# One visit of small tiles instead of two, and an earlier norm, in the last stage of a fused four-layer kernel

## The chip, the cores and the metric

The kernel runs as one program on one core of one Trainium2 chip. The metric is the device time of an execution in microseconds (us). The core's engines are TensorE (PE in the profile, with its weight loads as PEld), VectorE (DVE), ScalarE (ACT), GpSimd (POOL) and SyncE (SP), whose queue issues most of the transfers.

## The reference

Four layers follow each other on 4096 tokens (64 sequences of 64) of width 256. All are conditioned on one vector of 64 per sequence, here `t`.

```python
x = L0(x, t)     # quantized feed-forward
x = L1(x, t)     # attention, then the gated feed-forward below
x = L2(x, t)     # layer norm, scale and bias with a tanh term
x = L3(x, t)     # adapter whose weights depend on t

# second half of L1
h = gamma(t) * rmsnorm(x) + beta(t)
x = x + alpha(t) * ((silu(h @ gate_w.T) * (h @ hidden_w.T)) @ out_w.T + out_b)
# L2
out = (x - mean) * rsqrt(var + 1e-5) * weight + bias + tanh(t @ lin_w.T + lin_b)
x = out * weight + bias
# L3, with its own 128x256 and 256x128 matrices for each sequence
Wd_b = Wd + 0.1 * (t @ Wdd.T + bdd)
Wu_b = Wu + 0.1 * (t @ Wdu.T + bdu)
x = x + relu(x @ Wd_b.T + bd) @ Wu_b.T + bu
```

The feed-forward of L1 has 1024 hidden units. Its products are made from pairs of rounded high and low parts, three matmuls for each (`mm3`, lines 83 to 85).

## The kernel before, in words

The kernel has three stages: L0, attention, and a last stage that holds the feed-forward of L1 together with L2 and L3. The change lies in the last stage alone. The order of the work on PE, ACT, DVE and POOL is the order in which the program is written. SP's transfers are placed by a planner, which keeps each within its dependences.

The last stage works on eight blocks (`NBLK`) of 512 tokens, which are eight sequences each. A block takes eight steps, one for each 128 hidden units. The loop at line 1032 runs over `n`, with `i` the block and `f` the step in it (`n = 8 * i + f`). Beside the feed-forward of block `i` it carries the work of the blocks before and after it:

- `f_inner(n)` makes the gate and hidden products ("gh", 12 matmuls of 512 columns), takes the Silu on ACT (L695) and multiplies on DVE (L696, "sg"). `f_parts(n)` splits the result into "hhi" (ACT, L717) and "hlo" (DVE, L718). `f_outer(n - 2)` adds the output products of two steps before to "acc" (12 matmuls of 256 columns).
- For the next block: `f_load` (L658) brings its tokens, `f_begin` takes the squares (ACT, L210) and the inverse root of their means (POOL, L201 and L203), `f_scale` scales the rows (ACT, L225, tile "xn"), and `norm_turn` transposes them on PE (L234), multiplies on DVE (L237, "xg") and adds on POOL (L238). One step later the result is split into "xh" and "xl" (L217, L218). The turns stand in steps 5 and 6.
- For the block before: `f_scaled`, `f_added`, `f_stats` and `f_center` (L741, L746, L751, L752, L758, L760) do the residual and the layer norm in steps 1 and 2; `f_adapt` turns it in steps 4 and 5 (PE L794, DVE L795, tile "x4"). Then comes the adapter: `f_down` (PE L824, ACT relu L828, tile "dn") in step 6, `f_up_products` (PE L839) in step 7 and `f_up_store` (DVE L854, tile "yo", and the output transfer L856).
- `f_weights` loads the adapter's matrices ("wd" L771, "wu" L774) and `f_common` adds the common part to them on POOL (L785). `f_base` adds a bias row to the tokens on POOL (L679).

The adapter's products use only half of the array's columns at a time: 32 products of 64 tokens for the down half, 32 for the up half (each is two matmuls in the profile, 64 in all), all with `tile_position=(0, 64 * s)`. All other matmuls of the stage take the full array.

PSUM has eight banks: four for "gh", two for "acc", two for "mm". The two "mm" banks are taken in turn by the transposes and by the adapter's products. The tiles "dn" and "yo" have one buffer each, "wd" and "wu" four (two blocks). "x1" has five, which the loaded tokens and the layer norm's result share.

Two blocks differ. In block 0 there is no block before. In the last block there is no next one; the adapter of block 6 and all of block 7 are done in `f_last`, after the loop.

Of the kernel before, what the change touches and what calls it, by code (L numbers as in the profile page):

```python
# [8 lines left out]
F32 = mybir.dt.float32  # L9
# [8 lines left out]
P = 128  # L18
NB = 64
L = 64  # L20
D = 256
NTOK = NB * L
T = 512
NBLK = NTOK // T
# [3 lines left out]
BN = 128  # L28
# [8 lines left out]
def tile_kernel(ctx: ExitStack, tc, xT, x, condT, cw, upT, downT, qkvT, woT, ghT, outT_w,  # L37
                vecs, rows, g1, g2, gb, out):
    nc = tc.nc
# [8 lines left out]
    s1d = dram.tile([2, NB, 128, BN], F32, name="s1d")  # L48
    s2d = dram.tile([2, NB, 64, D], F32, name="s2d")
# [12 lines left out]
    def bank(tag):  # L62
        uid[0] += 1
        tags = pools["tags"]
        if tag not in tags:
            tag = "mm"
        return pools["ps"].tile([P, 512], F32, tag=tag, bufs=tags[tag], name=f"{tag}_{uid[0]}")
# [6 lines left out]
    def block(name):  # L74
        return main.tile([P, TT, D], F32, tag="x1", bufs=X1, name=name)

    def tok(ap, i):

        return ap[i * T:(i + 1) * T, :].rearrange("(t p) d -> p t d", p=P)
# [126 lines left out]
    def rms(xb, name):  # L206
        ss = main.tile([P, TT], F32, tag="ss", bufs=2, name=f"ss{name}")
        for t in range(TT):
            junk = main.tile([P, D], F32, tag="junk", bufs=1, name=f"junk{name}_{t}")
            nc.scalar.activation(junk, xb[:, t], AF.Square, accum_out=ss[:, t:t + 1])  # L210
        return rsqrt(ss, 1.0 / D, 1e-6, name)
# [8 lines left out]
    def norm_tm(xb, rs, name, scalar=False):  # L220

        xn = main.tile([P, TT, D], F32, tag="xn", bufs=1, name=f"xn{name}")
        for t in range(TT):
            if scalar:
                nc.scalar.activation(xn[:, t], xb[:, t], AF.Copy, scale=rs[:, t:t + 1])  # L225
            else:
                nc.vector.tensor_scalar(xn[:, t], xb[:, t], rs[:, t:t + 1], None, ALU.mult)
        return xn, parts(name)
# [427 lines left out]
    def f_load(i):  # L656
        x2 = block(f"fx2_{i}")
        nc.sync.dma_start(out=x2, in_=tok(x2d, i))  # L658
        fblk[i] = dict(x2=x2)

    def f_begin(i):
        fblk[i]["rs"] = rms(fblk[i]["x2"], f"f{i}")

    def f_scale(i):
        fblk[i]["n"] = norm_tm(fblk[i]["x2"], fblk[i]["rs"], f"f{i}", i > 0)
# [88 lines left out]
    def f_center(i, tiles, rs):  # L754

        B, n, t0 = fblk[i], len(tiles), tiles[0]
        nm = pools["c"].tile([P, TT], F32, tag="nm", bufs=2, name=f"nm{i}_{t0}")
        nc.vector.scalar_tensor_tensor(nm[:, :n], B["mv"][:, t0:t0 + n, 0], -1.0, rs[:, :n], ALU.mult, ALU.mult)  # L758
        for k, t in enumerate(tiles):
            nc.scalar.activation(B["x3"][:, t], B["x3"][:, t], AF.Identity, bias=nm[:, k:k + 1], scale=rs[:, k:k + 1])  # L760

    def f_weights(i):

        pool = pools["c"]
        B = fblk[i]
        B["wd"], B["wu"] = [], []
        for k in range(2):
            bs = slice(i * BB + 4 * k, i * BB + 4 * k + 4)
            wd = pool.tile([P, 4, 2, BN], F32, tag="wd", bufs=4, name=f"wd{i}_{k}")
            for c in range(2):  # L770
                nc.sync.dma_start(out=wd[:, :, c, :], in_=s1d[c, bs].rearrange("b d n -> d b n"))  # L771
            wu = pool.tile([P, 4, D], F32, tag="wu", bufs=4, name=f"wu{i}_{k}")
            for s in range(2):
                nc.sync.dma_start(out=wu[s * 64:(s + 1) * 64], in_=s2d[s, bs].rearrange("b n d -> n b d"))  # L774
            B["wd"].append(wd)
            B["wu"].append(wu)

    def f_common(i, which, k):

# [35 lines left out]
    def f_down(i, half=None):  # L815
        B = fblk[i]
        if half in (None, 0):
            B["dn"] = pools["c"].tile([P, T], F32, tag="dn", bufs=1, name=f"dn{i}")
        b0, b1 = (0, BB) if half is None else (half * BB // 2, (half + 1) * BB // 2)
        pd = bank("mm" if half is None else "acc")  # L820
        for b in range(b0, b1):
            for c in range(2):
                for s in range(2):
                    nc.tensor.matmul(pd[s * 64:(s + 1) * 64, (b - b0) * L:(b - b0 + 1) * L],  # L824
                                     lhsT=B["wd"][b // 4][:, b % 4, c, s * 64:(s + 1) * 64],
                                     rhs=B["x4"][:, c, b * L:(b + 1) * L], start=c == 0, stop=c == 1,
                                     tile_position=(0, 64 * s))
        nc.scalar.activation(B["dn"][:, b0 * L:b1 * L], pd[:, :(b1 - b0) * L], AF.Relu, bias=vc[:, 5, 0:1])  # L828

    def f_up_products(i, half=None):  # L830
        B = fblk[i]
        b0, b1 = (0, BB) if half is None else (half * BB // 2, (half + 1) * BB // 2)
        pus = []
        for c in range(2):
            pu = bank("mm" if half is None else "gh")
            for b in range(b0, b1):
                for s in range(2):
                    o = c * P + s * 64
                    nc.tensor.matmul(pu[s * 64:(s + 1) * 64, (b - b0) * L:(b - b0 + 1) * L],  # L839
                                     lhsT=B["wu"][b // 4][:, b % 4, o:o + 64],  # L840
                                     rhs=B["dn"][:, b * L:(b + 1) * L], start=True, stop=True,
                                     tile_position=(0, 64 * s))
            pus.append(pu)
        return pus

    def f_up_store(i, pus, half=None):
        B = fblk[i]
        if half in (None, 0):
            B["yo"] = pools["c"].tile([P, 2, T], F32, tag="yo", bufs=1, name=f"yo{i}") if i + 1 < NBLK else \
                main.tile([P, 2, T], F32, tag="xn", bufs=1, name=f"yo{i}")  # L850
        yo, n = B["yo"], T if half is None else T // 2
        o = 0 if half is None else half * n
        for c in range(2):
            nc.vector.scalar_tensor_tensor(yo[:, c, o:o + n], pus[c][:, :n], vc[:, 4, c:c + 1], B["x4"][:, c, o:o + n],  # L854
                                           ALU.add, ALU.add)
            nc.sync.dma_start(out=out[c * P:(c + 1) * P, i * T + o:i * T + o + n], in_=yo[:, c, o:o + n])  # L856
# [86 lines left out]
    for w in range(W):  # L943
        i, tp = divmod(w, 2)
# [86 lines left out]
    late = []  # L1031
    for n in range(5, N):
        i, f = divmod(n, 8)
        ahead = 0 < i < NBLK - 1

        for rest in late:
            rest()
        late = []
        if i > 0 and f == 2:
            f_added(i - 1, 1)  # L1040
            f_stats(i - 1, 1)
            rln = rsqrt(fblk[i - 1]["mv"][:, :, 1], 1.0, 1e-5, f"ln{i - 1}")
        sg = f_inner(n)
        if i > 0 and f in (4, 5):
            f_adapt(i - 1, f - 4)
        if i + 1 < NBLK and f in (5, 6):
            late = [norm_turn(*fblk[i + 1]["n"], i + 1, f - 5, V_FG, V_FB)]
        if ahead and f == 6:
            f_down(i - 1)
        if ahead and f == 7:  # L1050
            pus = f_up_products(i - 1)
        f_parts(n, sg)
        f_outer(n - 2) if n > 5 else None
        if ahead and f == 7:
            f_up_store(i - 1, pus)
        if n == 6:
            for k in range(2):
                nc.vector.scalar_tensor_tensor(bias[:, k], gbt[:, 2 * k + 1], 0.1, gbt[:, 2 * k], ALU.mult, ALU.add)
        if i > 0:
            if f == 1:  # L1060
                for k in range(2):
                    f_scaled(i - 1, k)
                f_added(i - 1, 0)
                f_stats(i - 1, 0)
            if f == 2:
                f_center(i - 1, range(TT), rln)
        if f == 2 and i > 0:
            f_rows(i)
            if i + 1 < NBLK:
                f_load(i + 1)  # L1070
        if i > 0 and i + 1 < NBLK:
            if f == 3:
                f_begin(i + 1)
            if f == 4:
                f_scale(i + 1)

        if f == (6 if i + 1 < NBLK else 2):
            f_weights(i)
        if i + 1 < NBLK and f == 7:
            f_common(i, "wd", 0)  # L1080
            f_base(i)
        if i > 0 and f == 0:
            f_common(i - 1, "wd", 1)
        if i > 0 and f in (3, 4):
            f_common(i - 1, "wu", f - 3)
        if i + 1 == NBLK:
            if f == 4:
                f_base(i)
            if f in (5, 6):
                f_common(i, "wd", f - 5)  # L1090
                f_common(i, "wu", f - 5)
# [57 lines left out]
```

## Time and profile before

| | us |
|---|---|
| Median of three runs | 783.71 |
| Lowest and highest run | 780.1 and 784.03 |
| The profiled execution | 783.55 |
| Its span, from first to last instruction | 781.8 |
| PE busy | 755.3 (97% of the span) |
| DVE, ACT, POOL busy | 546.0, 398.0, 342.1 |
| The last stage from 474 us on: PE busy | 301.2 of 308.0 |

The granted TensorE clock is 0.995 in the mean. Matmuls overlap in the profile: [...]the next matmul starts earlier. So PE's busy share hides short waits, and the distance from start to start tells what a matmul costs the engine. A line of a timeline gives the start, the duration, engine, line and operation, output and inputs, shapes, and the number of instructions merged into it.

### The profile page before, as it was taken

To read this page: it belongs to the slowest core of one execution; us is meant where nothing else is said; L and a number is where in the kernel's file an instruction comes from. 1 tells how busy PE (TensorE), PEld (TensorE's weight loads), DVE (VectorE), ACT (ScalarE), POOL (GpSimd) and SP (SyncE) were. 2 spreads that over 40 slices of the span, in tenths; PEclk is the share of its full clock that TensorE was granted. 3 is DMA by queue.
4 is the path that set the end of the run, shared out by engine and by line. 5 is a ranking of instruction groups with operands and counts; after the bars stand their busy time and mean duration, and the time that the engine had idled before them with its cause. 6 is when DMAs were issued, how large, how long until landed. Compare 5 with 4: busy or idle time off the path is not lost. (4 is left out here: it accounts for less than half of the span.)

```text
span 781.8 us, 17390 instructions
## 1 busy us (share of the span) xinstructions
PE 755.3 (97%) x7014; PEld 615.7 (79%) x7014; DVE 546.0 (70%) x859; ACT 398.0 (51%) x818; POOL 342.1 (44%) x352
## 2 busy tenths in 40 slices
PE   4999999999999989999999999999999999999997
PEld 3677776776777878888788888888888888888886
DVE  4677687777678678998888886555655555464565
ACT  4624345344354478888778664434334352526242
POOL 4311121221324236666556416380818273645491
PEclk9998999999999999999999999999999999999999
DMA  9987988997974783554663137725161616161501
GB/s 322 273 154 215 269 230 223 292 211 208 284 195 117 174 191 84 141 141 139 150 150 92 42 115 176 162 65 152 55 162 55 162 56 162 55 163 33 157 1 55
DMA packets 117136, 118.87 MB, mean 152 GB/s; under 512 B 39568, under 2 KB 100624, under 8 KB 117056
## 3 DMA queue, kind: packets, MB, share of 16 engines
q1 hardware_dynamic: 109024, 91.35, 47.9%
q0 software_dynamic: 7488, 25.37, 9.1%
q8 instruction: 55, 0.90, 0.5%
q10 hardware_dynamic: 544, 1.05, 0.4%
q14 instruction: 25, 0.20, 0.1%
HBM read 71.41 MB, written 29.56 MB: 129 GB/s over the span
## 5 line engine op out<-in xcount | busy, mean ns | idle before, releaser
L83 PE MATMUL mm<-up,xhl 128*128 128x512 f32 x256 | 107.6, 420 | 2.2 <-ACT xhl L217 2.2
L696 DVE TENSOR_TENSOR sg<-gh,sg 128x512 f32<-128x512 f32 x61 | 42.0, 688 | 93.5 <-ACT sg L695 47.4
L84 PE MATMUL mm<-up,xhl 128*128 128x512 f32 x256 | 103.5, 404 | 0.5 <-DVE up L308 0.5
L85 PE MATMUL mm<-up,xll 128*128 128x512 f32 x256 | 102.9, 402 | 0.0
L83 PE MATMUL gh<-xhf,gh 128*128 128x512 f32 x244 | 97.2, 399 | 0.0
L84 PE MATMUL gh<-xlf,gh 128*128 128x512 f32 x244 | 96.9, 397 | 0.0
L85 PE MATMUL gh<-xhf,gh 128*128 128x512 f32 x244 | 96.9, 397 | 0.0
L374 ACT ACTIVATE g<-mm,rs_l 128x512 f32<-128x512 f32 x64 | 44.0, 689 | 90.0 <-PE mm L85 61.9
L718 DVE TENSOR_TENSOR hlo<-sg,hhi 128x512 fp32r<-128x512 f32 x61 | 63.1, 1035 | 37.0 <-ACT hhi L717 36.6
L717 ACT CAST hhi<-sg 128x512 fp32r<-128x512 f32 x61 | 37.8, 619 | 84.7 <-DVE sg L696 83.8
L375 DVE SCALAR_TENSOR_TENSOR h<-mm,rs_l,g 128x512 f32<-128x512 f32 x64 | 47.6, 746 | 44.6 <-PE mm L85 43.5
L83 PE MATMUL acc<-wout,hhi 128*128 128x256 f32 x256 | 74.9, 293 | 0.0
L85 PE MATMUL acc<-wout,hlo 128*128 128x256 f32 x256 | 72.4, 283 | 0.3 <-DVE hlo L718 0.2
L84 PE MATMUL acc<-wout,hhi 128*128 128x256 f32 x256 | 72.3, 282 | 0.0
L83 PEld LDWEIGHTS mm<-up,xhl 128*128 128x128 f32 x256 | 49.4, 193 | 25.6 <-DVE am L383 4.9
L695 ACT ACTIVATE sg<-gh 128x512 f32<-128x512 f32 x61 | 36.0, 590 | 53.2 <-PE gh L85 53.2
L85 PEld LDWEIGHTS mm<-up,xll 128*128 128x128 f32 x256 | 49.2, 192 | 12.3 <-DVE xll L218 0.5
L84 PEld LDWEIGHTS mm<-up,xhl 128*128 128x128 f32 x256 | 49.4, 193 | 11.5 <-DVE up L308 1.2
L238 POOL TENSOR_TENSOR xg<-xg,cv 128x512 f32<-128x512 f32 x32 | 35.8, 1127 | 43.7 <-DVE xg L237 43.7
L85 PEld LDWEIGHTS gh<-xhf,gh 128*128 128x128 f32 x244 | 46.1, 189 | 10.8
L84 PEld LDWEIGHTS gh<-xlf,gh 128*128 128x128 f32 x244 | 46.3, 190 | 8.1
L83 PEld LDWEIGHTS gh<-xhf,gh 128*128 128x128 f32 x244 | 46.3, 190 | 8.1
(188 smaller groups left out, 1879.7 us busy)
## 6 DMA issues: line engine op xcount, KB each, us to landing
gt<-in_g SPq DMA_DIRECT2D x32, 512.0 KB, 5.6
rows<-alphad SPq DMA_DIRECT2D x48, 256.0 KB, 4.2
s1d<-stg POOLq DMA_DIRECT2D x32, 256.0 KB, 6.7
s2d<-stg POOLq DMA_DIRECT2D x32, 256.0 KB, 6.5
vb<-vx SPq DMA_DIRECT2D x32, 256.0 KB, 4.7
wd<-s1d SPq DMA_DIRECT2D x32, 256.0 KB, 4.2
wu<-s2d SPq DMA_DIRECT2D x32, 256.0 KB, 5.8
xf<-in_xT SPq DMA_DIRECT2D x8, 512.0 KB, 3.8
```

Of the source, the lines that this page charges most:

```text
L83: nc.tensor.matmul(out, lhsT=l[0], rhs=r[0], start=first, stop=False)
L84: nc.tensor.matmul(out, lhsT=l[0], rhs=r[1], start=False, stop=False)
L85: nc.tensor.matmul(out, lhsT=l[1], rhs=r[0], start=False, stop=last)
L238: nc.gpsimd.tensor_tensor(b3(xg), b3(xg), bc(vb, c, i), ALU.add)
L374: nc.scalar.activation(g, pg, AF.Gelu, scale=rs[:, t:t + 1])
L375: nc.vector.scalar_tensor_tensor(h[:, ch * 512:(ch + 1) * 512], pv, rs[:, t:t + 1], g, ALU.mult, ALU.mult)
L695: nc.scalar.activation(sg, pg, AF.Silu)
L696: nc.vector.tensor_tensor(sg, pv, sg, ALU.mult)
L717: nc.scalar.copy(h_hi, sg)
L718: nc.vector.tensor_tensor(h_lo, sg, h_hi.bitcast(F32), ALU.subtract)
```

## The change

It has two parts, both in the loop at line 1032.

The norm of the next block moves ahead: its load from step 2 to step 0, its squares from step 3 to step 1, its scales from step 4 to step 3. The two turns stay in steps 5 and 6.

The adapter's two halves share a place: in step 7 of block `i` PE makes half of the up products of block `i - 2`, then the down products of block `i - 1`, then the other half of the up products. The up half is thus a block later than before. `f_up_products` gets a function that it calls between its halves, and `f_up_store` can store one half. The last up half of the loop (block 5) comes in step 0 of block 7. The weight loads are parted: "wd" in step 6 and "wu" in step 7, and in the last block both in step 1 instead of step 2.

```diff
-    def f_weights(i):
+    def f_weights(i, which):
...
-    def f_up_products(i, half=None):
+    def f_up_products(i, half=None, between=lambda pus: None):
...
             pu = bank("mm" if half is None else "gh")
+            pus.append(pu)
             for b in range(b0, b1):
...
-            pus.append(pu)
+            if c == 0:
+                between(pus)
         return pus
 
-    def f_up_store(i, pus, half=None):
+    def f_up_store(i, pus, half=None, chunks=range(2)):
...
-        for c in range(2):
+        for c in chunks:
...
-        ahead = 0 < i < NBLK - 1
+        more = i + 1 < NBLK
...
-        if i + 1 < NBLK and f in (5, 6):
+        if more and f in (5, 6):
             late = [norm_turn(*fblk[i + 1]["n"], i + 1, f - 5, V_FG, V_FB)]
-        if ahead and f == 6:
+        up = i - 2 if more and f == 7 else i - 2 if not more and f == 0 else -1
+        if up >= 0:
+
+            def between(pus):
+                f_up_store(up, pus, chunks=range(1))
+                if more:
+                    f_down(i - 1)
+            pus = f_up_products(up, between=between)
+            f_up_store(up, pus, chunks=range(1, 2))
+        elif more and i > 0 and f == 7:
             f_down(i - 1)
-        if ahead and f == 7:
-            pus = f_up_products(i - 1)
         f_parts(n, sg)
         f_outer(n - 2) if n > 5 else None
-        if ahead and f == 7:
-            f_up_store(i - 1, pus)
...
+        if i > 0 and more:
+            if f == 0:
+                f_load(i + 1)
+            if f == 1:
+                f_begin(i + 1)
+            if f == 3:
+                f_scale(i + 1)
         if f == 2 and i > 0:
             f_rows(i)
-            if i + 1 < NBLK:
-                f_load(i + 1)
-        if i > 0 and i + 1 < NBLK:
-            if f == 3:
-                f_begin(i + 1)
-            if f == 4:
-                f_scale(i + 1)
-
-        if f == (6 if i + 1 < NBLK else 2):
-            f_weights(i)
-        if i + 1 < NBLK and f == 7:
+
+        if f == (6 if more else 1):
+            f_weights(i, "wd")
+        if f == (7 if more else 1):
+            f_weights(i, "wu")
+        if more and f == 7:
             f_common(i, "wd", 0)
             f_base(i)
```

More of the change, by code (lines that the diff above doesn't have):

```diff
@@ L760, in f_center @@
             nc.scalar.activation(B["x3"][:, t], B["x3"][:, t], AF.Identity, bias=nm[:, k:k + 1], scale=rs[:, k:k + 1])
-    def f_weights(i):
+    def f_weights(i, which):
         pool = pools["c"]
         B = fblk[i]
-        B["wd"], B["wu"] = [], []
+        B[which] = []
         for k in range(2):
             bs = slice(i * BB + 4 * k, i * BB + 4 * k + 4)
-            wd = pool.tile([P, 4, 2, BN], F32, tag="wd", bufs=4, name=f"wd{i}_{k}")
-            for c in range(2):
[L771 to L776, printed above, removed]
+            if which == "wd":
+                w = pool.tile([P, 4, 2, BN], F32, tag="wd", bufs=4, name=f"wd{i}_{k}")
+                for c in range(2):
+                    nc.sync.dma_start(out=w[:, :, c, :], in_=s1d[c, bs].rearrange("b d n -> d b n"))
+            else:
+                w = pool.tile([P, 4, D], F32, tag="wu", bufs=4, name=f"wu{i}_{k}")
+                for s in range(2):
+                    nc.sync.dma_start(out=w[s * 64:(s + 1) * 64], in_=s2d[s, bs].rearrange("b n d -> n b d"))
+            B[which].append(w)
     def f_common(i, which, k):
@@ L842, in f_up_products @@
                                      tile_position=(0, 64 * s))
-            pus.append(pu)
+            if c == 0:
+                between(pus)
         return pus
-    def f_up_store(i, pus, half=None):
+    def f_up_store(i, pus, half=None, chunks=range(2)):
         B = fblk[i]
-        if half in (None, 0):
+        if half in (None, 0) and chunks[0] == 0:
             B["yo"] = pools["c"].tile([P, 2, T], F32, tag="yo", bufs=1, name=f"yo{i}") if i + 1 < NBLK else \
@@ L852, in f_up_store @@
         o = 0 if half is None else half * n
-        for c in range(2):
+        for c in chunks:
             nc.vector.scalar_tensor_tensor(yo[:, c, o:o + n], pus[c][:, :n], vc[:, 4, c:c + 1], B["x4"][:, c, o:o + n],
@@ L1085, in tile_kernel @@
             f_common(i - 1, "wu", f - 3)
-        if i + 1 == NBLK:
+        if not more:
             if f == 4:
```

## The prediction

> **What bounds the kernel now.** Names: step f of block i is one pass of the last loop (n = 8i + f); a *visit* is a stretch in which TensorE leaves the full array for the 128x64 tiles of L824 (down) or L839 (up). I read the page for the whole, then the table of busy times by stretch for the last stage, cut at the starts of one block's step 7 to the next:
>
> ```profile
> PE 755.3 (97%) x7014; PEld 615.7 (79%) x7014; DVE 546.0 (70%) x859; ACT 398.0 (51%) x818; POOL 342.1 (44%) x352
> ...
> 520.60:561.30 40.70, 40.56 (x338) 35.16 (x337) 21.85 (x35) 16.75 (x35) 20.92 (x19) 1.00 0.39 104
> 561.30:602.00 40.70, 40.56 (x338) 35.16 (x337) 21.82 (x35) 16.76 (x35) 20.92 (x19) 1.00 0.40 102
> ```
>
> A block takes 40.7 us and PE is busy for 40.56 of it, while DVE has 21.8, ACT 16.8, POOL 20.9. Only what TensorE issues, or waits for, sets the stage. Busy time hides short waits, since matmuls overlap; so next the waits of the weight loads from 485 us on:
>
> ```profile
> PEld mm L234 <- ACT xnf L225: 3.1, 12, 0.3
> PEld mm L839 <- issue: 2.2, 6, 0.4
> ...
> PEld mm L824 <- POOL xg L238: 1.0, 6, 0.2
> ```
>
> The first is the wait that the norm's move aims at; the other two recur six times at the entry of visits. Their true price is in start times, in PE's timeline. An undisturbed turn of the norm, a stalled one (step 5), a down visit (step 6), an up visit (step 7):
>
> ```profile
> 477.92 0.60 PE L234 MATMUL mm<-ident,xnf 128*128 128x128 f32 x4
> 478.27 0.36 PE L83 MATMUL acc<-wout,hhi 128*128 128x256 f32 x1
> 478.48 0.28 PE L84 MATMUL acc<-wout,hhi 128*128 128x256 f32 x1
> ...
> 549.55 1.21 PE L234 MATMUL mm<-ident,xnf 128*128 128x128 f32 x4
> 550.51 0.36 PE L83 MATMUL acc<-wout,hhi 128*128 128x256 f32 x1
> ...
> 554.82 0.60 PE L234 MATMUL mm<-ident,xnf 128*128 128x128 f32 x4
> 555.35 2.09 PE L824 MATMUL mm<-x,wd 128*64 128x64 f32 x64
> 557.36 0.38 PE L83 MATMUL acc<-wout,hhi 128*128 128x256 f32 x1
> 557.59 0.28 PE L84 MATMUL acc<-wout,hhi 128*128 128x256 f32 x1
> ...
> 561.46 0.39 PE L85 MATMUL gh<-xhf,gh 128*128 128x512 f32 x1
> 561.78 2.08 PE L839 MATMUL mm<-dn,wu 128*64 128x64 f32 x64
> 563.80 0.38 PE L83 MATMUL acc<-wout,hhi 128*128 128x256 f32 x1
> 564.02 0.28 PE L84 MATMUL acc<-wout,hhi 128*128 128x256 f32 x1
> ```
>
> The 64 small matmuls follow each other at (2.09 - 0.22) / 63 = 0.0297 us (the last one's own length taken off), 1.90 us in all. The rest of a visit is entry and exit.
>
> **What the Trainium skill says.** "TensorEngine Tiling (Array Packing)", Key Properties: changing the tiling mode, unlike changing the tile, drains TensorE. The trace agrees: entry comes 0.32 us after the last gh start where gh follows gh after 0.23, and the first two acc matmuls after a visit are 0.22 apart instead of 0.12. Up and down both use the 128x64 mode, so between them no drain is due. "SBUF — State Buffer", Who interferes with whom: a VectorE instruction with two SBUF inputs contends with a GpSimd one that reads SBUF. The trace agrees: hlo (L718) takes 0.69 us alone and 1.29 to 1.73 beside POOL's bias adds (L785). "TensorE: Matmul & The Clock Gate", Architectural detail: ScalarE and VectorE are strict first-in, first-out. The trace agrees: xhf (L217) waits 2.98 us for POOL at 555.22 and the Silu behind it starts right after.
>
> **The change, part by part.**
>
> *Norm earlier.* The squares (L210, four, 2.04 us with their reads) go from step 3 to step 1, the scales (L225, four, 1.70 us) from 4 to 3, the load from 2 to 0; nothing is added. The stalled turn takes 550.51 - 549.55 = 0.96 us, the undisturbed one 478.27 - 477.92 = 0.35. Twelve waits are two in each of six turns: 6 x 0.61 = **3.6 us off PE**. Cover for the moved work: between steps 1 and 2 ACT idles 1.48 us ahead of the Silu and 4.04 ahead of hhi, while DVE does the statistics; 2.04 us of squares make that Silu 0.56 late, of 4.04. The scales, in the place of the squares at 544.77, end near 546.5, 3 us ahead of the turn. POOL's ms and rs of the norm (1.2 us) now stand ahead of ms_ln, for which POOL idles 10.86 us.
>
> *Two visits in one.* Step 6 loses its down visit: from turn to second acc 557.59 - 554.82 = 2.77 us becomes 478.48 - 477.92 = 0.56, so -2.21, six times. Step 7 in blocks 2 to 6 gains 64 small matmuls without entry or exit, +1.90 (five times); in block 1 it holds a down in place of an up, 0. Block 7 gains an up visit in step 0: 564.02 - 561.46 = 2.56 against 0.36 for a plain gh to second acc (0.24 + 0.12), +2.20. Sum: -13.3 + 9.5 + 2.2 = **-1.6 us**.
>
> *New waits, and what stands behind them.* Let V be a visit's start.
> - The second up half takes the PSUM bank of the first ("mm" has two), so PE waits for DVE's first yo (L854). That can start at V + 0.95 + 0.19 + 0.04 = 1.18 (products, last one's end, hand-over as at L828), after sg, which ends at V + 0.87 (561.96 + 0.69 - 561.78); it takes 0.74 and ends at V + 1.92. PE wants the bank at V + 0.95 + 1.90 = 2.85. Slack 0.9 us: nothing.
> - "dn" has one buffer, so the relu (L828) waits for the second up half, to V + 4.0, and hhi and hlo of step 7 stand behind it on ACT and DVE, to V + 7.1 at the longest hlo. Their acc products come two steps later: 3.8 + 0.15 + two acc groups of 1.44 + two gh groups of 2.80 = V + 12.4. Slack 5 us.
> - SP: the wd loads no longer wait for a down visit (118.7 us in six waits now); wu waits for the up visit instead, leaves at about V + 4 to 7 and lands 5.8 us later, while POOL touches it after rs_ln at V + 19. The next block's load stands behind it, still most of a block ahead of its squares, against a landing of 7.9 us. In the first block the load of block 2 precedes gbt and waits for a store issued at 448.91; gbt is used at 481.46. The block-7 weights move from step 2 to 1, and are touched in step 5. All nothing.
> - POOL's wu adds (5.5 us) move from beside steps 4 and 5 to beside 2 and 3, where they meet hlo of step 2: it may take 0.9 us more, and nm, centring, Silu of steps 3 and 4 and x4 (L795) follow. The step-5 turn takes the bank that x4 frees: now 548.03 + 0.74 = 548.77 against 549.55, slack 0.78. The scales are 0.34 us shorter than the squares whose place in ACT they take, so 0.78 + 0.34 - 0.9 = 0.2 us is left. This is the tightest place. Bounds: 0, or up to 0.5 us a turn if hlo and Silu lose more, 6 x 0.5 = 3.0. I take 0.
>
> Sum: 783.55 (profiled execution; 781.8 span and 1.75 around it) - 3.6 - 1.6 = **778.4 us**. The median of the runs, 783.71, lies 0.16 above that execution, so the ratio is 0.993 either way. A measurement of this kernel can tell about 0.5% (3.9 us) from no change; the limit is 779.8.
>
> **The rivals.**
> - *The turn waits for DVE instead of ACT* (the last bullet). For it: 0.2 us of slack. Against: hlo's delay is once a block. 778.4 + 3.0 = 781.4.
> - *The norm isn't earlier in fact*: its load or squares run late behind what SP holds, and the scales end where they did. For it: one queue, with a block's weights ahead. Against: the lead of most of a block. Only the visits gain: 782.0.
> - *Slower: the merged visit starves on its bank.* If DVE ends the first yo after V + 2.85, PE stands in the middle of each of five visits. The gain is gone when it ends 0.9 + 5.2 / 5 = 1.9 us later than reckoned. With hlo of step 6 (1.73) running into V and sg behind it, 2.8 late: 5 x 1.9 = 9.5, giving 787.9. Against: now hlo of step 6 ends over 2 us ahead of V.
>
> **How the numbers follow.** Forecast 0.62; bank of the turn 0.20; norm not earlier 0.10; starved visit 0.06; the rest unnamed. The first, and little else, is faster by over 0.5%: 0.64. The two middle ones and part of the forecast's edge are within 0.5%: 0.29. Slower: 0.07. Range: the three runs of before reach 3.6 us below their median, so down to 775.0; upwards it takes in both middle cases, to 782.5. The starved visit is left out.
>
> **What would show it.** Right: a block of 39.8 us between step-7 visits (40.7 - 0.61 - 0.31); no wait of L234 on L225; in step 7 one unbroken stretch of 128 small matmuls, 3.8 us, followed by an acc group. Wrong: L234 waiting on L795, or L839 on L854; small matmuls slower than 0.0297 us where up and down meet; a wait of acc on hlo in steps 0 to 2; or a time above 782.5.

## The result, and the profile after

The changed kernel takes 779.23 us in the median of 20 runs (773.96 to 782.29), beside 782.02 us for 20 runs of the kernel before (776.9 to 784.96). The ratio is 0.9959, with a 95% interval of 0.9944 to 0.9974: 3.2 us faster, between 2.0 and 4.4. Forecast were 778.4 us and a ratio of 0.993. Run again beside other runs of the kernel before, it gave 0.9953 (0.9933 to 0.9973). So the change makes the kernel faster, by about six tenths of the 5.2 us reckoned.

The profiled execution of the changed kernel took 774.54 us with a span of 772.8. That can't be set against the 781.8 of before as it stands. In all profiled kernels of this study PE has the same work in the same order up to the start of block 1 (n = 8), and yet block 1 starts anywhere between 479.1 and 485.7 us. Most of the difference between these two executions goes with TensorE's clock near the start of the program. In that of before the first 512-column matmuls follow each other at 0.43 us until 19.3 us and at 0.23 behind that, and the granted clock is 0.50 from 56.8 to 63.6 us; in that of the changed kernel the change comes at 14.4 us, and the clock is 0.50 from 55.4 to 58.8. So it ran for 8.2 us less at about half the speed. That is worth some 4.1 us (an estimate from these figures) of the 5.0 by which its block 1 starts earlier. So I compare distances inside the last stage, which repeat within 0.02 us a block.

First the busy line of the page, then the table by stretch (length, then PE, PEld, DVE, ACT and POOL, clock, DMA share, GB/s), cut at the merged visits of blocks 2 and 3:

```profile
PE 747.4 (97%) x7014; PEld 612.3 (79%) x7014; DVE 548.1 (71%) x859; ACT 397.4 (51%) x818; POOL 343.9 (45%) x352
```

```profile
551.38:591.16 39.78, 39.78 (x337) 34.96 (x336) 22.37 (x35) 16.67 (x35) 21.13 (x19) 1.00 0.45 107
```

A block takes 39.79 us in place of 40.65, as forecast (39.8), and PE shows no idle time in it: it still sets the pace. The longest waits of the weight loads from 478 us on:

```profile
PEld mm L841 <- issue: 2.2, 6, 0.4
PEld acc L825 <- issue: 1.7, 2, 0.8
PEld mm L841 <- POOL rs_ln L203: 0.9, 1, 0.9
```

The wait of L234 on L225, 3.1 us in twelve waits, is gone, and so is that at the entry of six down visits (1.0 us); six entries with up products stay. The wait on POOL's rs_ln is in the tail, where PE is in truth held by the relu behind the down products: it ends at 759.03, and the up products start at 759.13. Next PE's timeline, the turn of step 5 and the merged visit of step 7:

```profile
541.93 0.63 PE L234 MATMUL mm<-ident,xnf 128*128 128x128 f32 x4
542.31 0.36 PE L83 MATMUL acc<-wout,hhi 128*128 128x256 f32 x1
...
551.06 0.39 PE L85 MATMUL gh<-xhf,gh 128*128 128x512 f32 x1
551.38 1.15 PE L841 MATMUL mm<-dn,wu 128*64 128x64 f32 x32
552.37 2.04 PE L825 MATMUL mm<-x,wd 128*64 128x64 f32 x64
554.23 1.10 PE L841 MATMUL mm<-dn,wu 128*64 128x64 f32 x32
555.27 0.38 PE L83 MATMUL acc<-wout,hhi 128*128 128x256 f32 x1
555.49 0.28 PE L84 MATMUL acc<-wout,hhi 128*128 128x256 f32 x1
```

The turn goes from 541.93 to 542.31, 0.38 us where it was 0.96. The visit is one stretch of 128 small matmuls: 32 up, 64 down, 32 up, from 551.38 to 555.27, that is 3.89 with the exit. From up to down and from down to up the last start and the next are 0.05 us apart: next to nothing is lost where the two meet. Entry (0.32) and the two starts after the exit (0.22 apart) are as before, once a block in place of twice.

### The profile page after: what moved, and what is told of

Read it like the earlier page. It is cut to its first block, busy times and chain, and to the rows that moved or that the text cites. A ratio compares the mean times of both kernels' runs of the same rounds, so it can differ in the third digit from the quotient of the medians.

```text
span 772.8 us, 17369 instructions
## 1 busy us (share of the span) xinstructions
PE 747.4 (97%) x7014; PEld 612.3 (79%) x7014; DVE 548.1 (71%) x859; ACT 397.4 (51%) x818; POOL 343.9 (45%) x352
## 4 chain that ended last, share of the span: by engine, by line
PE 91%; DVE 4%; issue 2%; ACT 1%; DMA 1%; POOL 0%; SPq 0%; DVEq 0%
PE mm L83 12%; PE mm L84 11%; PE mm L85 11%; PE gh L83 7%; PE gh L84 7%; PE gh L85 7%; PE acc L83 4%; PE mm L273 4%; PE acc L85 4%; PE mm L400 4%; PE acc L84 4%; PE mm L591 2%; PE S L550 2%; PE mm L234 2%; PE mm L610 2%
## 5 line engine op out<-in xcount | busy, mean ns | idle before, releaser
L83 PE MATMUL mm<-up,xhl 128*128 128x512 f32 x256 | 106.4, 416 | 2.2 <-ACT xhl L217 2.2
L84 PE MATMUL mm<-up,xhl 128*128 128x512 f32 x256 | 102.1, 399 | 0.5 <-DVE up L308 0.5
L718 DVE TENSOR_TENSOR hlo<-sg,hhi 128x512 fp32r<-128x512 f32 x61 | 58.6, 960 | 31.3 <-ACT hhi L717 30.3
L85 PEld LDWEIGHTS mm<-up,xll 128*128 128x128 f32 x256 | 48.4, 189 | 12.1 <-DVE xll L218 0.5
```

Of the source, the lines that this page charges most:

```text
L83: nc.tensor.matmul(out, lhsT=l[0], rhs=r[0], start=first, stop=False)
L84: nc.tensor.matmul(out, lhsT=l[0], rhs=r[1], start=False, stop=False)
L85: nc.tensor.matmul(out, lhsT=l[1], rhs=r[0], start=False, stop=last)
L718: nc.vector.tensor_tensor(h_lo, sg, h_hi.bitcast(F32), ALU.subtract)
```

## The experiments

The distances below are from the traces. A step's length is taken from its first gate product to the next step's first; step 5 and step 7 are those of block 2; "blocks 1 to 6" is the sum of the six; the end is the distance from the start of the last matmul to the end of the span.

| kernel | step 5 | step 7 | blocks 1 to 6 | block 7, step 0 | end | ratio to before (95%) |
|---|---|---|---|---|---|---|
| before | 5.71 | 6.43 | 243.92 | 4.24 | 3.83 | |
| changed | 5.18 | 8.30 | 236.86 | 6.43 | 4.61 | 0.9959 (0.9944 to 0.9974) |
| norm_only | 5.17 | 6.43 | 240.65 | 4.24 | 3.62 | 0.9959 (0.9944 to 0.9974) |
| visits_only | 5.71 | 8.30 | 240.02 | 6.43 | 4.60 | 0.9996 (0.9976 to 1.0015) |
| split_up | 5.71 | 6.67 | 245.66 | 4.30 | 3.77 | 1.0023 (1.0007 to 1.0038) |
| tail_up | 5.16 | 8.30 | 236.77 | 4.24 | 3.45 | 1.0118 (1.0086 to 1.015) |
| begin_early | 5.10 | 6.43 | 240.25 | 4.24 | 4.07 | 0.996 (0.9944 to 0.9976) |
| store_two | 5.17 | 8.31 | 236.84 | 6.43 | 4.73 | 0.9933 (0.9905 to 0.9962) |
| tail_six_two | 5.16 | 8.31 | 236.85 | 4.24 | 3.51 | 0.9978 (0.9962 to 0.9994) |
| late_yo | 5.16 | 9.33 | 241.94 | 6.43 | 4.40 | 0.9996 (0.9978 to 1.0015) |
| scale_four | 5.11 | 8.30 | 236.43 | 6.43 | 3.96 | 0.9947 (0.9932 to 0.9963) |
| after_again | 5.16 | 8.30 | 236.82 | 6.43 | 4.11 | 0.9953 (0.9933 to 0.9973) |
| more_loads | 5.17 | 8.30 | 236.81 | 6.43 | 4.94 | a single run |

**norm_only: the norm's move alone.** The kernel before with

```diff
+        if i > 0 and i + 1 < NBLK:
+            if f == 0:
+                f_load(i + 1)
+            if f == 1:
+                f_begin(i + 1)
+            if f == 3:
+                f_scale(i + 1)
         if f == 2 and i > 0:
             f_rows(i)
-            if i + 1 < NBLK:
-                f_load(i + 1)
-        if i > 0 and i + 1 < NBLK:
-            if f == 3:
-                f_begin(i + 1)
-            if f == 4:
-                f_scale(i + 1)
```

> Only the norm's move: load in step 0, squares in step 1, scales in step 3; the visits stay as in the kernel before. Theory (the two parts add up, the norm is worth 0.52 to 0.61 us a block): a block goes from 40.65 to about 40.1 us, steps 5 from 5.71 to 5.1 to 5.2, no wait of L234 on the scales, and the kernel is 3.1 to 3.6 us faster than before (ratio about 0.9957). Rival (the wait only ended because the merged visit gave DVE and ACT another order): step 5 stays at 5.7 and the time stays within 1 us of before.

Step 5 fell to 5.17, a block to 40.11, the six blocks by 3.27 us; the ratio says 3.2 us. The move works alone, and takes 0.545 us a block off PE, not 0.61.

**visits_only: the merged visit alone.** The changed kernel with the norm's three calls back in steps 2, 3 and 4.

> Only the merged visit: the norm's load, squares and scales are put back to steps 2, 3 and 4. Theory: step 5 stays at 5.7 us with its wait; blocks 2 to 6 lose 0.31 us each, block 1 loses 2.2, block 7 gains 2.2, so 1.6 us faster than before in the trace (ratio about 0.998). Rival (the last block pays 0.8 us more because of the up visit in step 0 and what it delays): 0.8 us faster only, and the stretch from the last matmul to the end is again about 0.8 us longer than before, as in the changed kernel (4.4 against 3.6 us).

The six blocks lose 3.90 us and step 0 of block 7 gains 2.19: -1.71 us, near the -1.6 reckoned. The last step gives some of it back: PE waits 0.7 us there for an hlo (0.37 more than in the changed kernel), and the end is 4.60. In the time nothing can be seen: the interval reaches from -1.9 to +1.2 us. The two parts add: -3.27 - 1.71 = -4.98, against -7.06 + 2.19 = -4.87 with both.

**split_up: the price of one visit.** The kernel before with its up visit in two:

```diff
+        f_parts(n, sg)
         if ahead and f == 7:
-            pus = f_up_products(i - 1)
-        f_parts(n, sg)
-        f_outer(n - 2) if n > 5 else None
-        if ahead and f == 7:
+            pus = f_up_products(i - 1, between=lambda: f_outer(n - 2))
             f_up_store(i - 1, pus)
+        else:
+            f_outer(n - 2) if n > 5 else None
```

> The kernel before with its up visit of step 7 cut in two: the first 32 small matmuls, then the acc group, then the other 32. One more entry and exit for each of six blocks, no other work. Theory (a visit costs its entry and exit, 0.31 us beside its matmuls): step 7 goes from 6.43 to about 6.74 us, 1.9 us slower than before in all (ratio 1.0024). Rival (the price of a visit is the wait for its operands, not the change of tiling): step 7 stays within 0.1 us of 6.43.

Step 7 grew by 0.24 and the step behind it by 0.06: 0.30 us for one entry and exit with no other work, 1.74 us over the six blocks, and the ratio gives 1.8. So the 0.31 that the merged visit saves is the change of tiling, not a wait for operands.

**begin_early: which of the moved calls mattered.** The kernel before with only f_load in step 0 and f_begin in step 1; f_scale stays in step 4.

> The kernel before with only the load and the squares of the norm moved ahead (steps 0 and 1); the scales stay in step 4. Theory (what made the turn late was ACT's queue: 2.04 us of squares ahead of the Silu of step 4, so that the scales behind it ended 0.6 us too late): with the squares gone the scales of step 4 end about 1.9 us earlier by themselves, step 5 falls to about 5.17 us as it did with the whole move, 3.2 us faster than before (ratio 0.9957). Rival (it is the place of the scales that counts): step 5 stays at 5.7 us, same time as before.

The turn's stall is gone without touching the scales: step 5 is 5.10, its floor of a plain step and two turns (4.24 + 2 x 0.43), and the six blocks lose 3.67 us, as much as was reckoned for the whole move. ACT's timeline shows why. First the kernel before, then this one; step 5 of block 3 starts at 586.96 and at 586.75:

```profile
587.45 0.58 ACT L695 ACTIVATE sg<-gh 128x512 f32<-128x512 f32 x1
588.79 0.62 ACT L717 CAST hhi<-sg 128x512 fp32r<-128x512 f32 x1 [0.76 <-DVE sg L696]
589.32 1.71 ACT L225 ACTIVATE xnf<-fx,rs_f 128x256 f32<-128x256 f32 x4
```

```profile
586.31 0.59 ACT L695 ACTIVATE sg<-gh 128x512 f32<-128x512 f32 x1
587.76 0.62 ACT L717 CAST hhi<-sg 128x512 fp32r<-128x512 f32 x1 [0.86 <-DVE sg L696]
588.29 1.70 ACT L225 ACTIVATE xnf<-fx,rs_f 128x256 f32<-128x256 f32 x4
```

The scales ended 4.07 us after the step's start before, and 3.24 now, when the turn starts: just in time. The squares had stood ahead of the Silu of step 4 on ACT, and everything behind them was late.

**scale_four: the changed kernel with f_scale in step 4.**

```diff
-            if f == 3:
+            if f == 4:
                 f_scale(i + 1)
```

> The changed kernel with the scales of the norm back in step 4; load and squares stay in steps 0 and 1. Theory (with the squares gone the scales are early enough in step 4, and in step 3 they push the work behind them on ACT and DVE, and with it the first x4, so that the turn of step 5 waits for its bank): step 5 falls from 5.17 to 5.19 to about 5.10 us, 6 x 0.08 = 0.5 us faster than the changed kernel, 0.5% faster than before with what that has. Rival (in the changed kernel POOL's bias adds stand elsewhere than in the kernel before, so the scales of step 4 are late again, or the bank wait has another cause): step 5 stays at 5.17 us or more.

Step 5 is 5.11 and a block 39.71: 0.43 us off the six blocks. What holds the turn of the changed kernel instead of the scales is seen in its timeline, in step 5 of block 3 (starts at 578.43):

```profile
577.99 1.71 ACT L225 ACTIVATE xnf<-fx,rs_f 128x256 f32<-128x256 f32 x4
...
579.60 0.58 ACT L695 ACTIVATE sg<-gh 128x512 f32<-128x512 f32 x1
580.21 0.69 DVE L696 TENSOR_TENSOR sg<-gh,sg 128x512 f32<-128x512 f32 x1 [1.40 <-ACT sg L695]
580.82 0.74 DVE L796 SCALAR_TENSOR_TENSOR x<-mm,w,cv 128x512 f32<-128x512 f32 x1
...
581.71 0.63 PE L234 MATMUL mm<-ident,xnf 128*128 128x128 f32 x4
```

The scales in step 3 hold up the Silu of step 4, that the sg, that the x4, which ends at 581.56. The turn takes the bank that x4 has read, starts 0.15 us later, and so 3.28 us into the step, where it starts at 3.24 in begin_early. This is the best version of the study: in the trace it is 0.43 us a stage ahead of the changed kernel, and its ratio to before is 0.9947; that it beats the changed kernel the times can't tell (the intervals overlap).

**late_yo: the slack of the second up half.** The changed kernel with hhi and hlo ahead of the first yo:

```diff
             def between(pus):
+                f_parts(n, sg)
                 f_up_store(up, pus, chunks=range(1))
...
-        f_parts(n, sg)
+        if up < 0:
+            f_parts(n, sg)
```

> The changed kernel with hhi and hlo of the step put ahead of the first yo addition, on ACT and DVE, in each merged visit. It tests the slack of 0.9 us that the second up half has. Theory (PE wants the bank 2.85 us after the visit's start; the first yo ended at 1.96 and now comes behind hhi of 0.62 and hlo of 0.69 to 1.6 us, so at 3.0 to 4.0): PE stands 0.2 to 1.1 us in the middle of each of five visits, step 7 goes from 8.30 to 8.5 to 9.4 us, 1 to 5.5 us slower than the changed kernel. Rival (the bank is not what PE would wait for): step 7 stays at 8.30 us.

PE stands in each of five visits, in the waits of the weight loads and in PE's timeline:

```profile
PEld mm L841 <- DVE yo L857: 4.8, 5, 1.0
```

```profile
555.28 1.15 PE L841 MATMUL mm<-dn,wu 128*64 128x64 f32 x32
556.26 2.04 PE L825 MATMUL mm<-x,wd 128*64 128x64 f32 x64
559.11 1.15 PE L841 MATMUL mm<-dn,wu 128*64 128x64 f32 x32 [0.81 <-DVE yo L857]
```

The second half starts 3.83 us after the visit's start, in place of 2.85. Step 7 is 1.03 longer, the blocks 5.1 us in all; the time is that of the kernel before. The first yo ends 3.78 us into the visit, 1.82 later than in the changed kernel, and PE stands for 0.98 of it. So the slack of 0.9 us that the prediction gave this wait is real and needed: one instruction pair more ahead of the yo on DVE's queue costs the gain. In the changed kernel the yo runs from 552.59 to 553.34, 1.96 us into the visit, as reckoned (1.92).

**tail_up: the odd up visit after the loop.** The changed kernel with

```diff
-        up = i - 2 if more and f == 7 else i - 2 if not more and f == 0 else -1
+        up = i - 2 if more and f == 7 else -1
...
         f_down(i - 1)
+        f_up_store(i - 2, f_up_products(i - 2))
```

in `f_last`, and "dn" of block 6 in a buffer of the sg.

> The changed kernel with the up products of block 5 moved from step 0 of block 7 to after the loop, between the down and the up products of block 6, in the visit that is there in any case, where PE waited 0.8 us for the relu. Theory: step 0 of block 7 falls from 6.43 to 4.24 us; the visit in the tail grows by 1.9 us of small matmuls less the 0.8 us of wait; so about 1.1 us faster than the changed kernel, and nearly 4.3 us faster than before (ratio 0.9945). Rival (the tail is bound by DVE and ACT, and two more yo additions of 0.74 us each on DVE push the turns back): the gain of 2.2 us in step 0 is lost again in the tail, same time as the changed kernel. In either case, if the 0.8 us at the end come from the visit in step 0, the end is back to 3.6 us.

Both were wrong: it is 1.2% slower than before. Step 0 gained its 2.19, and the last step with the tail went from 24.09 to 39.13 us. The longest waits from 740 us on:

```profile
POOL wu L786 <- DMA wu<-s2d: 19.8, 1, 19.8
ACT x L760 <- DVE nm L758: 16.6, 2, 14.7
PEld gh L807 <- ACT x L760: 12.6, 2, 12.2
```

"wu" has buffers for two blocks. Block 5's, now read after the loop, are those that the load of block 7 needs; POOL stands for that load with the bias adds at the head of its queue, the layer norm's root behind them, and PE for the layer norm. Behind that wait the granted clock was at 0.50, from 764.4 to 781.5 us: the two down groups took 2.1 us each, where the changed kernel has 1.38, and the last 64 up products 2.70 in place of 2.04. That is another 2.1 of the 15 us. I had counted engines and forgotten who holds the buffers.

**tail_six_two: down and up in step 6 of block 7.** The changed kernel with

```diff
-        up = i - 2 if more and f == 7 else i - 2 if not more and f == 0 else -1
+        up = i - 2 if f == (7 if more else 6) else -1
```

the load of block 7's "wu" behind that visit, its adds in `f_last` (one before the first root, one after the second), no down products of block 6 there, and the transfers of store_two.

> The changed kernel with the up products of block 5 and the down products of block 6 in one visit in step 6 of block 7 (so none in step 0, and only the up products of block 6 are left after the loop), the up weights of block 7 loaded behind that visit and their bias added beside the layer norm of block 7; and the last transfers on two queues as in the run of that name. The last up products wait for nothing else. Theory: step 0 loses 2.19 us, step 6 gains 3.8 + 0.31; after the loop PE loses the 0.83 us wait for the relu and 1.9 us of down products, but the first turn then waits for the layer norm, so that it starts about 2.2 us earlier than now; net 0.3 us, with the two queues 1.0 to 1.4 us faster than the changed kernel. Rival (the up weights of block 7 come late again, as they did when the up products of block 5 stood after the loop and held their buffers): the last up products wait for POOL, and the kernel is 1 to 6 us slower than the changed one.

The up weights came in time and the last up products did not wait for them, and still it is 3.7 us longer in the stage than the changed kernel. The table by stretch (the eighth figure is the granted clock):

```profile
760.00:762.00 2.00, 1.75 (x61) 1.61 (x56) 1.83 (x6) 0.00 (x0) 0.79 (x2) 1.00 0.00 0
762.00:764.00 2.00, 0.67 (x4) 0.45 (x4) 1.54 (x6) 1.09 (x2) 0.32 (x3) 1.00 0.00 0
764.00:766.00 2.00, 1.38 (x22) 1.15 (x22) 1.68 (x3) 0.04 (x1) 2.00 (x3) 0.59 0.00 0
766.00:768.00 2.00, 2.00 (x22) 1.43 (x19) 0.00 (x0) 1.52 (x3) 1.13 (x1) 0.50 0.00 0
```

The last step's hlo now ran beside the moved wu adds and took 1.64 us, so that PE stood 0.8 us for it. With less work left for it, PE then waited 1.4 us for the layer norm, and from about 764.4 us on the clock was halved. It stayed so to the end of PE's work: the last 64 up products took 3.63 us in place of 2.04, the two down groups 2.11 each in place of 1.38, 3.1 us together. In the changed kernel the tail's 758 to 766 us are busy to 5.9 of 8 us and keep the full clock. The Trainium skill, "TensorE: Matmul & The Clock Gate", Part 1: The HAM clock gate, tells of the halving after an idle window of some 3.4 us. Here it came with no single gap over 1.5 us: of the 4 us from 760 on PE was busy for 2.4.

**store_two, more_loads and after_again: what the end costs.** The changed kernel ends 4.61 us after its last matmul starts, the kernel before 3.83. In the row of SP's output transfers the issue of one stands out (shortest, median and longest, ns), here of the changed kernel and then of its repetition, after_again:

```profile
L859 SPq DMA_DIRECT2D out_y<-yo x6: 351/389/1289, 766.1 to 769.9; - x6
```

```profile
L859 SPq DMA_DIRECT2D out_y<-yo x6: 356/391/754, 772.7 to 776.0; - x6
```

store_two gives two of the last four transfers to ACT:

```diff
-            nc.sync.dma_start(out=out[c * P:(c + 1) * P, i * T + o:i * T + o + n], in_=yo[:, c, o:o + n])
+            queue = nc.scalar if half is not None and c == 1 else nc.sync
+            queue.dma_start(out=out[c * P:(c + 1) * P, i * T + o:i * T + o + n], in_=yo[:, c, o:o + n])
```

> The changed kernel with two of the last four output transfers issued by ACT in place of SP. Theory (the 0.8 us that the changed kernel has more at its end is one transfer issue on SP of 1.29 us in place of 0.4 to 0.5, during which a packet of instructions is brought; behind it two more issues stand in line): with two queues the distance from the start of the last matmul group's last product to the end falls from 4.61 to 3.5 to 3.9 us, 0.7 to 1.1 us. Rival (the end is bound by the landing of the last transfer): the distance stays at 4.6 us.

No issue was longer than 0.47 us, the last was issued at 1.15 in place of 2.13 us, and the end came at 4.73 all the same: the last packets landed 2.3 us later, where it took 1.2 in the changed kernel. The rival holds. The ratio of 0.9933 comes from five runs; its interval (-7.4 to -3.0 us) takes in the -4.0 us of the trace and the changed kernel's ratio, so it shows no gain of its own.

more_loads cuts the load of gbt at the start of the stage into four, and after_again is the changed kernel itself.

> The changed kernel with the load of gbt at the start of the stage cut into four, so that SP issues three transfers more, 300 us ahead of the end; nothing else. It tests whether the 0.8 us at the end hang on where a packet of instructions falls. Theory (the packet comes at a fixed place in SP's stream): its start moves against the last output transfers, and the distance from the start of the last matmul to the end changes from 4.61 us to something between 3.5 and 4.7, with the long issue on another transfer or none. Rival (the 0.8 us belong to the merged visit or to chance): the third of the last issues stays at about 1.29 us and the distance at 4.6, or the place differs with no relation to the packet.

> The changed kernel once more, unedited, beside the two above. Theory (the blocks and the end are fixed by the program, the stretch ahead of the stage by the granted clock): blocks of 39.79 us within 0.02 us, the third of the last issues again at about 1.29 us and 4.61 us from the last matmul's start to the end, and a ratio near 0.995. Rival (the end is chance): the distance falls anywhere between 3.5 and 4.7 us.

In more_loads the same issue took 1.28 us and the end 4.94; the place doesn't hang on SP's count of transfers. In after_again the same issue took 0.75 and the end 4.11. So the place is the program's, and the size differs between executions of one kernel. In each of these traces and in those of scale_four and before one packet of 16 KB of instructions is under way during that issue, and it lasts 1.54 us in the changed kernel, 1.64 in more_loads, 1.24 in after_again, 0.98 in scale_four and 0.88 in before; the issue ends 0.2 to 0.4 us after it. Its length and the end go together in these five (4.61, 4.94, 4.11, 3.96, 3.83). That doesn't make it the cause: in store_two the packet took 0.88 us, as in before, and the end was 4.73. What goes with the end, roughly, in all six is the landing of a transfer that is issued ahead of the long issue, in 0.34 to 0.36 us (the second of the six): it took 3.9 us in the changed kernel and in more_loads, 4.0 in store_two, 3.4 in after_again, 3.2 in scale_four and 3.1 in before. So the transfers already under way are slow too.

Nor is the size all chance. In the seven traces with an up visit in step 0 of block 7 the end is 3.96 to 4.94 us, 4.48 in the mean; in the six without one (tail_up and tail_six_two among them) it is 3.45 to 4.07, 3.71 in the mean. Part of it seems to come with that visit, but no run parts the two. Whose instructions the packet holds, and what slows the transfers, stays open.

## Why the prediction was right

By its own steps, with the distances of the table:

- *Norm earlier*, -3.6: measured -3.27. The turn itself went from 0.97 to 0.38 (reckoned 0.96 to 0.35); 0.04 us of bank wait ahead of it, on x4, came in its place. This is the "tightest place" of the prediction, for which it took 0 between 0 and 3.0: the 0.2 us of slack were -0.04. The delay was 1.1 us and not 0.9, and its place was not the one named: hlo of step 2 stayed at 0.69, and nm (L758) was hit. In the kernel before, the norm's root stood between rs_ln and the wu adds on POOL. With the norm earlier, the adds follow at once and run beside nm. The row of nm on DVE (shortest, median and longest, ns), before and after:

```profile
L758 DVE SCALAR_TENSOR_TENSOR nm<-bmv,rs_ln x7: 156/156/1258, 500.1 to 744.0; 128x4 f32<-128x4 f32 x7
```

```profile
L758 DVE SCALAR_TENSOR_TENSOR nm<-bmv,rs_ln x7: 1253/1254/1257, 495.1 to 734.2; 128x4 f32<-128x4 f32 x7
```

  The two instructions in the changed kernel's timeline:

```profile
572.31 3.03 POOL L786 TENSOR_TENSOR wu<-wu,bias 128x512 f32<-128x512 f32 x2
572.85 1.25 DVE L758 SCALAR_TENSOR_TENSOR nm<-bmv,rs_ln 128x4 f32<-128x4 f32 x1
```

  Four columns of work take 1.25 us in place of 0.16, the centring waits for them, and the Silus of steps 3 and 4 behind the centring. The nm is long in all ten kernels whose squares are moved ahead, norm_only and begin_early among them, and short in the three others (before, visits_only and split_up), but for the last one of these, in block 7, where no next norm stands in between. No run takes the adds away alone, but this fits what the Trainium skill, "SBUF — State Buffer", section "Who interferes with whom", says of a VectorE instruction with two inputs in SBUF beside a GpSimd one that reads SBUF: nm ends at 574.11, when the first of the adds ends (574.09). Of the hlo times that the prediction puts beside L785 the longest, 1.73, stands beside POOL's base-row adds (L679); beside the wu adds (L785) alone hlo took 1.28 to 1.29 in blocks 1 to 6. That the scales in step 3 then added their own 1.7 us ahead of the Silu of step 4 is shown by scale_four; with the scales in step 4 the long nm costs the turn nothing (begin_early: step 5 at its floor).
- *Two visits in one*, -1.6: measured -1.71. Its terms: step 6 -2.20 (reckoned -2.21), step 7 +1.87 (+1.90), step 0 of block 7 +2.19 (+2.20). split_up measures the visit's own price apart, 0.30.
- *New waits*, all taken at nothing: right but for the 0.04. The relu waits for the second up half (4.6 us at the longest) and nobody needs it. late_yo shows that the rival of the starved visit was one placement away: 5.1 us in five visits.
- *The rivals.* "The turn waits for DVE instead of ACT" came true as a mechanism and was 0.04 us a turn in size, not 0.5. The norm was earlier in fact (norm_only). The visit didn't starve.
- *The sum*, -5.2, was mis-sized in two terms: the turn (0.06 us times six, 0.3), and the end of the program, which the sum didn't have (+0.8 in the profiled execution, +0.3 in the repetition, beside a before that varies as well). -4.87 and +0.78 make the -4.1 us of the trace; the times say -3.2 (-4.4 to -2.0) and -3.7 (-5.2 to -2.1). The median of 779.23 lies between 775.0 and 782.5, and only 0.8 above the forecast, but 1.7 us of that nearness is luck: in these runs the kernel before took 782.02, where the sum started from 783.71. And the most likely case, a gain of over 0.5% (given 0.64), is not what the medians show: 0.41% and 0.47% (with intervals that reach past 0.5%) lie in the case that was given 0.29, and the end of the program, which put them there in part, was named by no rival.

## What to carry to other kernels

When an engine is bound by stalls of tenths of a microsecond, follow the late operand back on the queue of the engine that makes it: here it was not the scales that were late but the squares two places ahead of them, and moving only those, with their load, gave the whole gain of the norm's part. Small tiles of one mode are worth keeping together, at 0.3 us a visit; but merging work of two blocks makes one block's results live longer, so ask first which buffers, banks and queues it holds (the first try at moving the odd visit lost 15 us, most of it by that). And before leaving an engine less work in a tail that waits for one result after the other, ask what clock it will have there.

## What the runs showed of the hardware

- TensorE's granted clock went to 0.50 in the tail after 4 us in which it was busy for 2.4, with no gap over 1.5 us, and stayed there for the 9 us to the end of its work, though 766 to 768 us was busy throughout (tail_six_two). In tail_up it went to 0.50 some 4 us into a wait of 12.1 us, and stayed there for 17 us.
- A VectorE instruction of 128x4 took 1.25 us beside a GpSimd add, and 0.16 without (nm, after and before).
- From the 128x64 up products to the 128x64 down products and back it is 0.05 us from start to start; leaving the full array and coming back costs 0.30 (split_up).
- One 16 KB packet of instructions, 0.88 to 1.64 us long, falls on the last output transfers. In five traces the end of the program comes up to 1.1 us later where it is longer, but not in store_two (0.88 us and an end of 4.73), so it is not shown to be the cause.
